# The last softmax chunk joins the row sums through an adding DMA; the additions around it change places in VectorE's queue

## The chip, the cores and the metric

The kernel runs on one core of a Trainium2 chip. The time is device microseconds (us) of one execution; several executions give a median. The profile is one further execution, recorded by the hardware profiler.

Engine names are those of the profile: PE is TensorE's matmul, PEld its weight load, DVE is VectorE, ACT is ScalarE, POOL is GpSimd, SP is SyncE. SP and POOL also issue the DMAs here. A queue name with a q (SPq, POOLq) is the part of an engine that issues instructions.

## The reference

The input is 16 images of 256 channels and 32x32 positions, in f32. Two layers follow each other, and each one does

```
x = x + attention(groupnorm(x))
```

The group norm has 16 groups along the last image axis, which the code treats as channels. The attention has 4 heads of 64 channels over 1024 tokens, and a position term made of queries:

```
q, k, v = Wq x + bq, Wk x + bk, Wv x + bv          # per head 64 x 1024
sim[i, j]  = q[:, i] . k[:, j]
qpos[i, j] = (rel_h + rel_w)[:, i] . q[:, j]
out        = v @ softmax(sim + qpos, axis=-1)^T
```

The layers have their own weights. Everything is computed in f32.

## The kernel before

**Units, blocks and chunks.** A unit is one layer of one image, 32 units in all; images alternate so that a layer of one is interleaved with a layer of another. A unit has four blocks, numbered b = 0 to 3: two pairs of heads, `pr`, by two halves of the 1024 queries, `half`. So b = 0 and 2 are *half-0 blocks*, and b = 1 and 3 are *half-1 blocks*. A block has eight chunks of 128 keys, j = 0 to 7. For each chunk:

- `seed` (L343, DVE) writes the position term, 128x1024, into a PSUM tile;
- `scores` (L379, PE) adds the product of keys and queries onto it, in 8 matmuls;
- the exponential (L388, ACT) leaves the probabilities in an SBUF tile `p`, 128x1024 f32.

`attend` (L413, PE) multiplies the probabilities by the values, in two stretches of 64 matmuls, `values_of_p(0)` and `values_of_p(1)`. Four PSUM tags of two banks each, a, b, c and d, carry everything; `ring` says which stage uses which. A seed can be written only when ACT has read what stood in its tag before.

**Row sums.** `add_up(blk, j)` (L397 for j = 1, L399 for j = 2 to 7, all on DVE) adds up the eight chunks of a block into a tile `acc`, 128x1024. The two last chunks of a block are partly added in the next block, where the code calls that block `previous`. Then, for all but the last four blocks (`folded`):

- `fold` (L432): an adding DMA, issued by POOL, adds partitions 64 to 127 of `acc` onto partitions 0 to 63 (256 KB);
- `stack_up` (L441): two plain DMAs, issued by SP, copy a quarter each into a tile `stack` (64 KB each);
- `fold_again` (L448): two adding DMAs, issued by POOL, add the next quarters onto them;
- `sums_of_pair` (L460, PE) forms the sums of a pair's two blocks at the end of the following half-0 block. ACT copies them (L475), SP sends them to `den_all` (L481), DVE takes reciprocals (L519), SP spreads those through DRAM over the partitions (L521, L526, tile `rden`), and `finish` (L538, L540, DVE) multiplies the output by them and adds bias and residual. `finish` runs in half-1 blocks only, before the seeds of the next block. In the second layer it also issues the output DMA (L542).

**Pieces.** Projections, values and position terms of the coming unit are cut into pieces and put between the chunks' scores: `first` and `second`, made by `prepare`. A piece has two stretches of matmuls, which use different rows of the array. Between two stretches stands a *word*: when the first stretch is done, POOL writes one element of a tile `token` (L163), and the second stretch waits for that. These words stand in POOL's queue in program order with the DMAs that POOL issues: the order there within a half-0 block is word of `first`, `fold`, word of `second`, `fold_again`, word of `attend`. In a half-1 block it is word of `first`, `fold`, word of `attend`, `fold_again`; the second piece of such a block has one stretch only.

**Group norm of the unit after the next.** ACT forms its sums and squares 1/16 at a time (`norm_sums`, `norm_squares`, L187, and `norm_apply`, L242), at written-out places between the exponentials. In block 3 `norm_var` ends with two small POOL operations (L231, L233). Every second unit or so, block 3 also loads an image (`load_x`, L106, 1 MB on SP's queue), 13 times in all after the start.

The order on every engine is the program's order: nothing is rearranged by a scheduler. PE's order of a block is scores 1 to 3 (their seeds were written in the block before), `first(0)`, scores 4, `second(0)`, `first(1)`, scores 5, `second(1)`, scores 6, scores 7, `values_of_p(0)`, scores 0 of the next block, `values_of_p(1)`. DVE's order of a half-1 block is add 7 of the previous block, seed 4, add 1, reciprocal, seeds 5, 6, 7, adds 2, 3, 4, seed 0 of the next block, add 5, `finish` (two operations), seeds 1, 2, 3 of the next block.

Of the kernel before, what the change touches and what calls it, by code (L numbers as in the profile page):

```python
# [13 lines left out]
ALU = mybir.AluOpType  # L14
# [5 lines left out]
G = 16  # L20
# [32 lines left out]
def fast_path(ctx, tc, sh, x, layers, out, W, den_all, token, good, flag):  # L53
# [26 lines left out]
    nc = tc.nc  # L80
    B, C, H, N, CC, NT, NH, D, GT = (
        sh.B, sh.C, sh.H, sh.N, sh.CC, sh.NT, sh.NH, sh.D, sh.GT
    )
# [19 lines left out]
    def load_x(b):  # L103
        xt[b] = xpool.tile([P, CC, N], F32, tag="x", name=f"x_{b}")
        for cc in range(CC):
            nc.sync.dma_start(xt[b][:, cc, :], flat(x[b, cc * P : (cc + 1) * P]))  # L106
# [39 lines left out]
    def psum2(tag, name):  # L146
        return ps_s.tile([P, 2, HALF], F32, tag=tag, name=name)
# [37 lines left out]
    def of_group(u, g, func, into, **bias):  # L185
        junk = small.tile([P, CC * sh.W, GT], F32, tag="junk", name=f"junk_{u}_{g}")
        nc.scalar.activation(  # L187
            junk, grouped(xt[units[u][0]], g), func, accum_out=into[:, g : g + 1], **bias
        )

    def norm_sums(u, gs):
        if u not in reds:
            reds[u] = small.tile([P, G], F32, tag="red", name=f"red_{u}")
        for g in gs:
            of_group(u, g, AF.Identity, reds[u])
# [26 lines left out]
    def norm_squares(u, gs):  # L222
        for g in gs:
            of_group(u, g, AF.Square, sums[u], bias=negs[u][:, g : g + 1])
# [14 lines left out]
    def norm_apply(u, gs):  # L239
        rstd, shift = rss[u]  # L240
        for g in gs:
            nc.scalar.activation(  # L242
                grouped(xns[u], g),
                grouped(xt[units[u][0]], g),
                AF.Identity,
                bias=shift[:, g : g + 1],
                scale=rstd[:, g : g + 1],
            )
# [87 lines left out]
    seeds, probs, accs, outs = {}, {}, {}, {}  # L336
# [18 lines left out]
    def widen(u, pr):  # L355

        r = W.rel[units[u][1]][:, pr, :]
        t = gnpool.tile([P, CC, N], F32, tag="gn", name=f"wide_{u}_{pr}")[:, 0, :]
        nc.vector.tensor_tensor(
            t.rearrange("p (w y) -> p w y", y=H),  # L360
            r[:, :H].unsqueeze(1).to_broadcast([P, sh.W, H]),
            r[:, H:].unsqueeze(2).to_broadcast([P, sh.W, H]),
            ALU.add,
        )
        wide[u, pr] = t

    def scores(blk, j, tag=None):

        u, pr, half = blk
        ps = psum2(tag, f"ps_{u}_{pr}_{half}_{j}") if tag else seeds.pop((blk, j))  # L370
        columns = slice(half * HALF, (half + 1) * HALF)
        for x, c in enumerate(QUARTERS):
            for h, hs in enumerate(QUARTERS):
                j0 = j * P + x * D
                terms = [(ks[u, pr], qs[u, pr])]
                if tag:
                    terms = [(qs[u, pr], wide[u, pr])] + terms
                for i, (a, b) in enumerate(terms):
                    nc.tensor.matmul(  # L379
                        ps[c, h, :],  # L380
                        a[hs, j0 : j0 + D],
                        b[hs, columns],
                        start=bool(tag) and i == 0,
                        stop=i == len(terms) - 1,
                        skip_group_check=True,
                    )
        p = ppool.tile([P, 2, HALF], F32, tag="p", name=f"p_{u}_{pr}_{half}_{j}")
        nc.scalar.activation(p, ps, AF.Exp, bias=W.shift)  # L388
        probs[blk, j] = p

    def add_up(blk, j):
        u, pr, half = blk
        if j == 0:
            return
        if j == 1:
            accs[blk] = apool.tile([P, 2, HALF], F32, tag="acc", name=f"acc_{u}_{pr}_{half}")
            nc.vector.tensor_tensor(accs[blk], probs[blk, 0], probs[blk, 1], ALU.add)  # L397
        else:
            nc.vector.tensor_tensor(accs[blk], accs[blk], probs[blk, j], ALU.add)  # L399
# [26 lines left out]
    R = P // 4  # L426
    stacks = {}

    def fold(blk):

        acc = accs[blk]
        nc.gpsimd.dma_start(acc[:D], acc[D:], accum_op=ALU.add)  # L432
# [185 lines left out]
    def block(n):  # L618
        blk = blocks[n]
        u, b = divmod(n, BPU)  # L620
        half = blk[2]
        before = blocks[n - 3][:2] if half == 1 and n > 2 else None
        after = blocks[n + 1] if n + 1 < len(blocks) else None
        previous = blocks[n - 1] if n > 0 else None
        one, two = u + 1 < NU, u + 2 < NU

        pieces = u + 1 < NU or b < 2
        if u + 1 == NU and b == 1:
            widen(u, 1)
        f0, f1, f2, f3 = ring  # L630
        folded = n - 1 < FOLDED
        if not pieces:
            return block_without_pieces(n, half)

        if previous:
            add_up(previous, 6 if half == 0 else 7)
        for j in range(1, 4):
            scores(blk, j)
        if b == 3 and u + 3 < NU and units[u + 3][0] not in xt:
            load_x(units[u + 3][0])  # L640
        (first, first_out), (second, second_out) = prepare(u, b)
        first(0)
        if b == 0 and one:
            norm_apply(u + 1, range(0, 1))
        if b == 2 and two:
            norm_sums(u + 2, range(8, 11))
        if b == 3 and two:
            norm_squares(u + 2, range(6, 9))
        seed(blk, 4, f1)
        if previous and half == 0:  # L650
            add_up(previous, 7)
        scores(blk, 4)
        add_up(blk, 1)
        if before:
            reciprocals(*before)
        if half == 0:
            add_up(blk, 2)
        if b == 0 and one:
            norm_apply(u + 1, range(1, 5))
        if b == 1 and one:  # L660
            norm_apply(u + 1, range(15, G))
        if b == 2 and two:
            norm_sums(u + 2, range(11, G))
        if b == 3 and two:
            norm_squares(u + 2, range(9, 13))
        second(0)
        if half == 1:
            second_out()
        first.word()
        if previous and folded:  # L670
            fold(previous)
            stack_up(previous)
        first(1)
        first_out()
        seed(blk, 5, f0)
        scores(blk, 5)
        if half == 0:
            add_up(blk, 3)
            second.word()
            if previous and folded:  # L680
                fold_again(previous)
            second(1)
            second_out()
        seed(blk, 6, f1)
        scores(blk, 6)
        if half == 0:
            ring[2:] = f3, f2
        seed(blk, 7, ring[2])
        scores(blk, 7)
        if half == 1:  # L690
            add_up(blk, 2)
            add_up(blk, 3)
        add_up(blk, 4)

        if after:
            seed(after, 0, f0)
        if n in check:
            next(checks)
        if b == 0 and one:
            norm_apply(u + 1, range(5, 10))  # L700
        if b == 3 and two:
            norm_squares(u + 2, range(13, G))
        po = psum2(ring[3], f"po_{n}")
        values_of_p = attend(blk, po)
        values_of_p(0)
        if two and b >= 2:
            mean, mean_out = (norm_mean if b == 2 else norm_var)(u + 2, zeroed(f1, f"pm_{n}"))
            mean(0)
        if after:
            scores(after, 0)  # L710
        values_of_p.word()
        if two and b >= 2:
            mean(1)
        if previous and folded and half == 1:
            fold_again(previous)
        if two and b >= 2:
            mean_out()
        add_up(blk, 5)
        if before:
            finish(*before)  # L720
        if half == 0:
            add_up(blk, 6)
        if after:
            for j in range(1, 4):
                seed(after, j, ring[j % 3])
        if b == 0 and one:
            norm_apply(u + 1, range(10, 15))
        if b == 1 and two:
            norm_sums(u + 2, range(0, 8))
        if b == 2 and two:  # L730
            norm_squares(u + 2, range(0, 6))
        values_of_p(1)
        if half == 1:
            take_out(blk, po)
            pos[n] = po
            return
        if n > 1:
            sums_of_pair(*blocks[n - 2][:2], po)
        take_out(blk, po, n > 1)
# [477 lines left out]
```

## Time and profile before

| what | value |
|---|---|
| median of 3 runs | 2670.57 us (2669.98 to 2670.76) |
| the profiled execution: its own time | 2669.75 us |
| the profiled execution: span of the trace | 2667.9 us |
| mean granted TensorE clock | 0.999 |
| PE busy | 2608.5 us (98%) |
| DVE busy | 2407.3 us (90%) |
| ACT busy | 1992.4 us (75%) |
| POOL busy | 466.5 us (17%) |
| chain that ended last | PE 56%, DVE 29%, ACT 8%, issue 5%, DMA 3% |

Busy time is the time in which an engine has an instruction under way. Matmuls overlap, and their ends are modelled, so a stretch of PE is best measured from the start of one group to the start of the next. The chain that ended last follows the work back from the end, at each step to whatever released it. In the timeline each row is a group of like instructions: start, duration from the first start to the last end, engine, line, operation, tiles and count, and in brackets the idle time before it with what ended it.

The trace is very regular: from the unit at 381 us on, the copies of the half outputs (L485) come again after 22.50, 17.78, 22.80 and 19.20 us, which makes 82.28 us per unit.

### The profile page before, as it was taken

The page shows a single profiled execution, that of the slowest core. Times are in us where ns is not written, and L with a number is a line of the kernel's source. Part 1 is how long each engine was busy: PE and PEld are TensorE (multiplying, and loading weights), DVE is VectorE, ACT ScalarE, POOL GpSimd, SP SyncE. Part 2 cuts the span into 40 slices and gives each one's busy share as a digit, 9 for nine tenths or more (in the row PEclk, how much of TensorE's full clock was granted, in tenths as well). Part 3 has the DMA queues.
Part 4 walks back from the last instruction along what each step waited for, and adds up shares of the span by engine and source line. Part 5 has one row for each costly group of instructions (what it writes and reads, how often), then busy time and mean ns, then how long its engine had stood idle before and what let it go on. Part 6 is the DMA issues. An engine that isn't in the chain of part 4 may idle for free.

```text
span 2667.9 us, 86560 instructions
## 1 busy us (share of the span) xinstructions
PE 2608.5 (98%) x37970; PEld 1412.8 (53%) x37970; DVE 2407.3 (90%) x2200; ACT 1992.4 (75%) x3996; POOL 466.5 (17%) x825
## 2 busy tenths in 40 slices
PE   8999999999999999999999999999999999999998
PEld 4555455555555555555545555455555555554554
DVE  7988988989989899898998998998989989899998
ACT  6778777787777777777777778777777777777754
POOL 1211211112112111121121111211112112111110
PEclk9999999999999999999999999999999999999999
DMA  2222231322322223222222222222222232222221
GB/s 80 36 58 44 40 73 34 69 52 36 73 40 67 49 35 77 44 59 50 53 61 42 58 51 62 52 42 58 55 58 51 42 68 47 49 43 47 50 51 46
DMA packets 76136, 140.26 MB, mean 53 GB/s; under 512 B 33896, under 2 KB 35432, under 8 KB 75752
## 3 DMA queue, kind: packets, MB, share of 16 engines
q0 software_dynamic: 21824, 48.78, 12.6%
q1 hardware_dynamic: 53928, 85.89, 11.2%
q8 instruction: 299, 4.90, 0.8%
q14 instruction: 85, 0.70, 0.1%
HBM read 51.78 MB, written 17.30 MB: 26 GB/s over the span
## 4 chain that ended last, share of the span: by engine, by line
PE 56%; DVE 29%; ACT 8%; issue 5%; DMA 3%; SPq 0%; POOL 0%; DVEq 0%; POOLq 0%
PE ps L379 18%; PE po L413 17%; DVE ps L343 11%; DVE acc L399 10%; PE pq L262 8%; PE pk L262 6%; PE pv L292 4%; DVE x L540 3%; DVE od L538 3%; ACT p L388 3%; ACT junk L187 2%; ACT abt L331 2%; DMA den_all<-od 2%; DVE acc L397 1%; PE po L460 1%
## 5 line engine op out<-in xcount | busy, mean ns | idle before, releaser
L388 ACT ACTIVATE p<-ps,shift 128x1024 f32<-128x1024 f32 x1024 | 1105.4, 1118 | 428.7 <-PE ps L379 264.3
L343 DVE TENSOR_TENSOR ps<-abt 128x1024 f32<-128x1024 f32 x1018 | 1219.9, 1226 | 221.1 <-ACT p L388 116.2
L379 PE MATMUL ps<-q,k 64*64 64x512 f32 x8192 | 1038.7, 598 | 28.6 <-DVE ps L343 22.9
L399 DVE TENSOR_TENSOR acc<-acc,p 128x1024 f32<-128x1024 f32 x768 | 936.6, 1220 | 16.6 <-ACT p L388 0.9
L413 PE MATMUL po<-p,v 64*64 64x256 f32 x16384 | 933.5, 377 | 0.0
L413 PEld LDWEIGHTS po<-p,v 64*64 64x64 f32 x16384 | 674.0, 133 | 289.6 <-issue 61.4
L379 PEld LDWEIGHTS ps<-q,k 64*64 64x64 f32 x8192 | 296.4, 132 | 500.6 <-DVE ps L343 334.6
L163 POOL MEMSET token<- 1x1 f32 x380 | 33.8, 89 | 1795.0 <-PE po L413 696.0
L448 POOL DMA_DIRECT2D stack<-acc x248 | 195.0, 921 | 303.0 <-DMA stack<-acc 267.8
L292 PE MATMUL pv<-Wv,xn 64*64 64x256 f32 x4096 | 247.2, 376 | 0.3 <-DVE var L865 0.3
L262 PE MATMUL pq<-xn,Wq 64*64 64x512 f32 x2048 | 243.4, 590 | 0.3 <-DVE xn L897 0.3
L262 PE MATMUL pk<-xn,Wk 64*64 64x512 f32 x2048 | 242.9, 589 | 0.0
L292 PEld LDWEIGHTS pv<-Wv,xn 64*64 64x64 f32 x4096 | 176.5, 133 | 80.4 <-issue 49.7
L242 ACT ACTIVATE xn<-x,nshift,rstd 128x128 f32<-128x128 f32 x496 | 210.4, 497 | 0.1
L187 ACT ACTIVATE junk<-x,neg 128x128 f32<-128x128 f32 x498 | 197.0, 407 | 1.0
L397 DVE TENSOR_TENSOR acc<-p,p 128x1024 f32<-128x1024 f32 x128 | 155.6, 1216 | 0.0
L262 PEld LDWEIGHTS pq<-xn,Wq 64*64 64x64 f32 x2048 | 78.6, 134 | 141.7 <-issue 140.1
L187 ACT ACTIVATE junk<-x 128x128 f32<-128x128 f32 x480 | 144.1, 306 | 2.6 <-DVE x L540 2.6
L262 PEld LDWEIGHTS pk<-xn,Wk 64*64 64x64 f32 x2048 | 75.5, 134 | 123.5 <-issue 115.3
L485 ACT COPY od<-po 128x512 f32<-128x512 f32 x127 | 74.7, 589 | 75.5 <-PE po L413 75.5
L432 POOL DMA_DIRECT2D acc<-acc x124 | 103.4, 834 | 71.9 <-DVE acc L399 41.5
L231 POOL TENSOR_TENSOR rstd<-var,mhalf 128x16 f32<-128x16 f32 x30 | 108.2, 3607 | 3.2
(78 smaller groups left out, 1060.0 us busy)
## 6 DMA issues: line engine op xcount, KB each, us to landing
rden<-rd SPq DMA_DIRECT2D x126, 256.0 KB
acc<-acc POOLq DMA_DIRECT2D x124, 256.0 KB, 3.6
x<-in_x_dram SPq DMA_DIRECT2D x32, 512.0 KB
stack<-acc SPq DMA_DIRECT2D x248, 64.0 KB
stack<-acc POOLq DMA_DIRECT2D x248, 64.0 KB, 2.6
out_dram<-x SPq DMA_DIRECT2D x31, 512.0 KB
den_all<-od SPq DMA_DIRECT2D x124, 4.0 KB
rd<-r SPq DMA_DIRECT2D x63, 8.0 KB
```

Source lines behind the costliest of these rows:

```text
L187: nc.scalar.activation(junk, grouped(xt[units[u][0]], g), func, accum_out=into[:, g : g + 1], **bias)
L231: nc.gpsimd.tensor_tensor(rstd, var, W.mhalf[:, :G], ALU.pow)
L242: nc.scalar.activation(grouped(xns[u], g), grouped(xt[units[u][0]], g), AF.Identity, bias=shift[:, g : g + 1], scale=rstd[:, g : g + 1],)
L262: yield nc.tensor.matmul(pk[c, nh, :], w[l][rs, cc, c0 : c0 + D], xns[u][rs, cc, nh * HALF : (nh + 1) * HALF], start=(t == 0 and cc == 0), ...
L292: yield nc.tensor.matmul(pv[c, a, i, :], xns[u][rs, cc, j0 : j0 + D], W.wv[l][rs, cc, :], start=(t == 0 and cc == 0 and i == 0), stop=(t = ...
L343: nc.vector.tensor_tensor(ps.rearrange("p h (w y) -> p h w y", y=H), ab[:, :, :H].unsqueeze(2).to_broadcast([P, 2, XH, H]), ab[:, :, H + h ...
L379: nc.tensor.matmul(ps[c, h, :], a[hs, j0 : j0 + D], b[hs, columns], start=bool(tag) and i == 0, stop=i == len(terms) - 1, skip_group_check ...
L388: nc.scalar.activation(p, ps, AF.Exp, bias=W.shift)
L397: nc.vector.tensor_tensor(accs[blk], probs[blk, 0], probs[blk, 1], ALU.add)
L399: nc.vector.tensor_tensor(accs[blk], accs[blk], probs[blk, j], ALU.add)
L413: yield nc.tensor.matmul(po[c, a, :QUART], vts[u][rs, j, c0 : c0 + D], p[rs, h, a * QUART : (a + 1) * QUART], start=(t == 0 and j == 0), s ...
L448: nc.gpsimd.dma_start(stacks[u, pr][r0 : r0 + R, :], acc[R:D, h, :], accum_op=ALU.add)
```

## The change

The eighth chunk of a block (j = 7) is no longer added by DVE, for all blocks but the last four: a new function `add_last` issues a DMA on POOL's queue that adds the whole tile `p` (128x1024, 512 KB) onto `acc`. It is issued at the start of the next block, after add 6 of the previous block, which in every block now opens DVE's work. The `fold` that follows reads what this DMA wrote.

The other additions move: add 2 stands between seeds 5 and 6 in every block, and adds 3 and 4 after seed 7. Before, in a half-0 block, add 2 stood ahead of seed 5, add 3 between seeds 5 and 6, and add 6 behind add 5; in a half-1 block adds 2, 3 and 4 all stood after seed 7. `finish` stays where it was relative to the seeds, behind add 5. On ACT two of the sixteen squares of block 3 move from ahead of `second_out` to behind the eighth exponential.

```diff
+    def add_last(blk):
+        nc.gpsimd.dma_start(accs[blk], probs[blk, NT - 1], accum_op=ALU.add)
+
...
         if previous:
-            add_up(previous, 6 if half == 0 else 7)
+            add_up(previous, 6)
+            if folded:
+                add_last(previous)
+            else:
+                add_up(previous, 7)
         for j in range(1, 4):
             scores(blk, j)
...
         seed(blk, 4, f1)
-        if previous and half == 0:
-            add_up(previous, 7)
         scores(blk, 4)
         add_up(blk, 1)
         if before:
             reciprocals(*before)
-        if half == 0:
-            add_up(blk, 2)
...
         if b == 3 and two:
-            norm_squares(u + 2, range(9, 13))
+            norm_squares(u + 2, range(9, 11))
...
         seed(blk, 5, f0)
         scores(blk, 5)
+        add_up(blk, 2)
         if half == 0:
-            add_up(blk, 3)
             second.word()
             if previous and folded:
                 fold_again(previous)
...
         seed(blk, 7, ring[2])
         scores(blk, 7)
-        if half == 1:
-            add_up(blk, 2)
-            add_up(blk, 3)
+        add_up(blk, 3)
         add_up(blk, 4)
...
         if b == 3 and two:
-            norm_squares(u + 2, range(13, G))
+            norm_squares(u + 2, range(11, G))
...
         add_up(blk, 5)
         if before:
             finish(*before)
-        if half == 0:
-            add_up(blk, 6)
         if after:
```

## The prediction

> **What bounds the kernel now.** I read the page first, for the busy shares, the chain that ended last and the DMA issues, then the timelines of one half-1 block (b = 3) on PE and DVE, and last POOL's timeline in the half-0 block before it.
>
> ```profile
> span 2667.9 us, 86560 instructions
> ...
> PE 2608.5 (98%) x37970; PEld 1412.8 (53%) x37970; DVE 2407.3 (90%) x2200; ACT 1992.4 (75%) x3996; POOL 466.5 (17%) x825
> ...
> PE 56%; DVE 29%; ACT 8%; issue 5%; DMA 3%; SPq 0%; POOL 0%; DVEq 0%; POOLq 0%
> ...
> acc<-acc POOLq DMA_DIRECT2D x124, 256.0 KB, 3.6
> ```
>
> PE looks full at 98%, yet DVE holds 29% of the chain: somewhere PE waits for it in small steps. PE's timeline shows where:
>
> ```profile
> 1089.57 1.09 PE L379 MATMUL ps<-q,k 64*64 64x512 f32 x8 [0.56 <-DVE ps L343]
> 1090.48 3.63 PE L413 MATMUL po<-p,v 64*64 64x256 f32 x64
> 1094.47 0.23 PE L207 MATMUL pm<-sum,avg 64*64 64x16 f32 x2 [0.36 <-DVE pm L199]
> ...
> 1095.47 3.68 PE L413 MATMUL po<-p,v 64*64 64x256 f32 x64
> 1099.12 3.36 PE L379 MATMUL ps<-q,k 64*64 64x512 f32 x24
> 1102.29 1.91 PE L292 MATMUL pv<-Wv,xn 64*64 64x256 f32 x32
> ```
>
> From start to start, unhindered groups take 0.86 us for a chunk's scores, 1.72 for a piece's stretch, 3.45 for half of attend, 0.93 for the position terms, 0.43 for the sums. Against those, PE loses 0.78 us before scores 7 (the group ahead, scores 5 and 6, began at 1087.07 and needed 1.72), 0.54 before the norm's `pm`, 0.20 before the three scores at 1099.12, and 0.59 inside them (3.17 where 2.58 are needed): **2.1 us** in block 3. In block 1 the same count gives 0.37 + 0.60 = **1.0 us**. The half-0 blocks between them have gaps of 0.1 us at most: they are bound by PE. So about 3.1 us of a unit's 82.28 can be had.
>
> DVE in the same block:
>
> ```profile
> 1085.84 1.23 DVE L343 TENSOR_TENSOR ps<-abt 128x1024 f32<-128x1024 f32 x1 [0.56 <-ACT p L388]
> 1088.28 1.23 DVE L343 TENSOR_TENSOR ps<-abt 128x1024 f32<-128x1024 f32 x1 [1.20 <-ACT abt L331]
> 1089.42 3.74 DVE L399 TENSOR_TENSOR acc<-acc,p 128x1024 f32<-128x1024 f32 x3
> 1093.08 1.23 DVE L343 TENSOR_TENSOR ps<-abt 128x1024 f32<-128x1024 f32 x1
> 1094.23 1.21 DVE L399 TENSOR_TENSOR acc<-acc,p 128x1024 f32<-128x1024 f32 x1
> ...
> 1097.81 3.52 DVE L343 TENSOR_TENSOR ps<-abt 128x1024 f32<-128x1024 f32 x3
> 1101.24 1.23 DVE L399 TENSOR_TENSOR acc<-acc,p 128x1024 f32<-128x1024 f32 x1
> ```
>
> DVE idles 1.76 us for seeds 6 and 7, then three additions hold back seed 0 of the next block, and everything behind it is late.
>
> [...] Back to back, starts are 1.14 us apart, which I use. [...] `fold` lands after 3.6 us alone, but `stack_up` starts 5.5 us after it (1084.47 to 1089.99) beside the reciprocals' spreading.
>
> **The change, part by part.**
>
> *DVE loses 124 additions,* 124 x 1.22 = 151 us of busy time. But block by block: a half-0 block had additions 6 and 7 of the previous and 1 to 6 of its own, and keeps six of these eight. A half-1 block has six before and six after (6 of the previous for 7). All that is removed lies in blocks that PE bounds: **worth nothing directly**; PE's work covers it.
>
> *The new order in the half-1 block is what pays.* Block 3, on the times above: seed 5 ends at 85.2; add 2 fills the gap to 86.35; seed 6 to 87.5 (0.5 later than before, hidden: PE scores 5 until 87.93). Seed 7 needs the copy of `abt`, which started at 1087.26 behind four squares of 0.39 us; two move behind it, so it ends 0.78 earlier, at 87.4. Seed 7: 87.5 to 88.64, in time for scores 7 at 88.79. Adds 3 and 4 end at 90.9, seed 0 at 92.1. PE then goes 89.65, attend to 93.1, `pm` and scores 0 to 94.1, attend to 97.55. DVE: add 5, `finish`, then seed 1 at 95.6 (`pm`'s tag must first be read by ACT), seed 3 ends 99.1, when scores 3 are due at 99.27. The next piece starts at 1100.1 instead of 1102.29: 2.1 us. Block 1, worked likewise: seed 0 about 1.0 earlier, gain 1.0. The moved squares fall into ACT's 2.38 us of idleness ahead of the next exponential: nothing. Some 30 units: 30 x 3.1 = **-93 us**.
>
> *124 DMAs of 512 KB are added.* POOL: 124 x 0.82 (`fold`'s row) = 102 us, in a queue that is 17% busy. Landing: the page gives 48.78 MB on that queue 12.6% of 16 engines' span, 336 us, so 0.5 MB takes 3.6 us and `fold`'s half 1.8; `fold` lands after 3.6, hence 5.4. From the sizes instead (64 KB 2.6, 256 KB 3.6) it is 4.9. I take **L = 5.15**. [...] the upper one is `fold`'s longest landing, 6.5, plus 1.6 = 8.1.
>
> *A wait is added:* `fold` now stands in POOL's queue until the new DMA has landed, and the word of `second` stands behind it. Before:
>
> ```profile
> 1062.55 0.09 POOL L163 MEMSET token<- 1x1 f32 x1 [7.63 <-PE pq L262]
> 1063.40 0.81 POOL L432 DMA_DIRECT2D acc<-acc  x1 [0.77 <-DVE acc L399]
> 1065.12 0.09 POOL L163 MEMSET token<- 1x1 f32 x1 [0.91 <-PE pk L262]
> 1069.35 1.57 POOL L448 DMA_DIRECT2D stack<-acc  x2 [4.13 <-DMA stack<-acc]
> ```
>
> In a half-0 block, from the start of scores 1: `second(1)` is due after 2.58 + 1.72 + 0.86 + 1.72 + 1.72 + 0.86 = 9.46 us. Add 6 ends after 2.7 to 2.8; the DMA starts 0.3 later; then L, and 1.2 for `fold`'s issue, the word and the signals. So the word is in time while L is below some **5.2**: a margin of nothing. I charge 0.3 us for blocks 0 and 2 together, 30 x 0.3 = **+9 us**. `fold_again` and the word of attend, moved later by the same chain, have over 1 us left, and the sums' use of `stack` 2 us. SP's `stack_up` gets later too; behind it stand only `den_all` and output stores, not due then. In half-1 blocks no word stands between `fold` and attend's, so POOL can wait.
>
> *DMA against DMA:* in 13 of the blocks 3 an image (1 MB) is loaded just when the new DMA runs; the reciprocals' trip (L521, L526) queues behind the image on SP. If the engines' times add, the trip lands 1.5 to 3 us later and `finish`, which has about 0.5 us to spare once the block is shorter, holds seeds 1 to 3. Nothing shows this overlap; from 0 to 2.5 us, I take 1.5: 13 x 1.5 = **+20 us**.
>
> Sum: -93 + 9 + 20 = -64 on the profiled execution's 2669.75 us (span 2667.9 and 1.85 around it); the median is 0.8 above that execution: **2606 us**.
>
> **The rivals.**
> 1. *The DMAs cost nothing* (L under 5, image loads overlap freely): 2670.6 - 93 = 2577 us. For it: the DMA engines are about a quarter busy. Against: the margin is nil.
> 2. *POOL's wait becomes the bound, and the kernel slower.* Each us of L beyond 5.15 stops PE for 1 us at `second(1)` in some 61 half-0 blocks. It decides from L = 5.15 + 93/61 = 6.7. At 8.1: 61 x 2.95 = 180 - 93, so 2758. For it: `fold` has taken 6.5. Against: it did so in half-1 blocks beside the reciprocals' spreading, which half-0 blocks don't have.
> 3. *Seed 7 stays behind ACT's copy,* or another release: then only one addition less lies ahead of seed 0, and block 3 gains 1.1 instead of 2.1: 30 us less, 2636.
> 4. That the additions were not worth removing because PE is at 98%: same time, 2670. Against: the gaps counted above.
>
> **How the numbers follow.** Forecast 0.55, rival 1 0.20, rival 3 0.10, rival 2 0.13 (a little of it within the bound), rival 4 0.02. A measurement of this kernel tells about 0.2%, 5.3 us, from no change. Faster 0.84, within 0.04, slower 0.12. The range goes from 2572, rival 1 with a little more, to 2655, rival 3 with L = 5.45 (18 us more); only rivals 2 and 4 and odd ends lie outside.
>
> **What would show it.** Right: blocks 1 and 3 near 17.7 and 18.3 us of PE work, `DVE ps L343` gone as an idle cause of PE, the new DMA landing near 5.2, DVE 150 us less busy. The token wait shows as PE idle for POOL L163 before the piece's second stretch; the image's cost as DVE waiting for `rden` in every second block 3. Wrong: PE waiting for words over 1.5 us per half-0 block, or the half-1 blocks as long as now.

## The result, and the profile after

The changed kernel takes **2683.35 us** (median of 10 runs, 2676.64 to 2691.70) against 2669.99 us for the kernel before (10 runs): ratio **1.0051** (95% interval 1.0039 to 1.0062). It is slower by half a per cent where 2606 us was forecast. The profiled execution took 2683.82 us, its span is 2682.0.

The page after, in the lines that answer to those of before:

```profile
span 2682.0 us, 86789 instructions
...
PE 2595.6 (97%) x37970; PEld 1410.4 (53%) x37970; DVE 2261.4 (84%) x2076; ACT 1986.3 (74%) x3996; POOL 565.7 (21%) x949
...
PE 61%; DMA 16%; DVE 10%; issue 5%; ACT 4%; POOL 2%; SPq 1%; DVEq 0%; POOLq 0%
...
acc<-p POOLq DMA_DIRECT2D x124, 512.0 KB, 4.7
```

DVE has lost its 146 us, and its share of the chain fell from 29% to 10%. What took its place stands in the same line: DMA went from 3% to 16%. The new DMA itself lands after 4.7 us, sooner than the 5.15 that the forecast took.

The time between the last copies of successive blocks (L485 before, L488 after) tells where the time went. All are us from the timelines, means over units 4 to 25; a unit with a load is one whose block 3 loads an image, and what that costs shows in the block 0 that follows.

| block | before | after |
|---|---|---|
| 0, following a load | 22.50 | 26.04 |
| 0, others | 22.49 | 22.64 |
| 1 | 17.79 | 18.47 |
| 2 | 22.81 | 22.14 |
| 3 | 19.20 | 18.14 |

Block 3 has its gain, and block 2 part of its own (in both, the seeds at the end of a half-1 block come earlier). Block 1 is longer, and the blocks 0 that follow a load lose 3.5 us each. The other blocks 0 do not lose, but they do not gain either, so that a unit without a load takes 81.4 us: 0.9 us less than before, where 3.1 were forecast. Where nothing disturbs it, PE's timeline from block 3 into block 0 is as forecast; here in a unit without a load:

```profile
1268.66 0.23 PE L207 MATMUL pm<-sum,avg 64*64 64x16 f32 x2
...
1269.67 3.66 PE L413 MATMUL po<-p,v 64*64 64x256 f32 x64
1273.14 2.77 PE L379 MATMUL ps<-q,k 64*64 64x512 f32 x24
1275.73 1.91 PE L292 MATMUL pv<-Wv,xn 64*64 64x256 f32 x32
```

The three scores take 2.59 us from start to start instead of 3.17, and attend runs on into them without a gap. The largest loss is in the units with a load. There SP, POOL, DVE and PE show one chain, each in its own timeline:

```profile
1170.14 0.90 SPq L106 DMA_DIRECT2D x<-in_x_dram  x2
1172.99 0.33 SPq L524 DMA_DIRECT2D rd<-r  x1
1179.52 1.19 SPq L529 DMA_DIRECT2D rden<-rd  x2
```

```profile
1170.83 0.89 POOL L430 DMA_DIRECT2D acc<-p  x1 [7.07 <-ACT p L388]
...
1179.60 0.83 POOL L435 DMA_DIRECT2D acc<-acc  x1 [6.80 <-DMA acc<-p]
```

```profile
1186.19 1.23 DVE L541 TENSOR_TENSOR od<-od,rden 128x1024 f32<-128x1024 f32 x1 [3.96 <-DMA rden<-rd]
```

```profile
1183.25 3.66 PE L413 MATMUL po<-p,v 64*64 64x256 f32 x64
1189.94 4.59 PE L379 MATMUL ps<-q,k 64*64 64x512 f32 x24 [3.03 <-DVE ps L343]
```

The image and the adding DMA start within 0.7 us of each other, and the latter takes 8.8 us instead of 4.9. The reciprocals' `rd`, 8 KB issued 2.2 us behind it, answers after 6.5 us, so `rden` is late, `finish` waits 3.96 us in DVE's queue, the seeds behind it are late, and PE stops for 3.03 us. Over the whole trace `finish` waits for `rden` 20 times, where it never did before, and PE's wait for seeds is twice the 22.9 us of before (us in total, times, longest):

```profile
DVE od L541 <- DMA rden<-rd: 53.6, 20, 4.5
PE ps L379 <- DVE ps L343: 45.6, 45, 3.6
```

And then PE's three scores take 4.59 us instead of 2.8. Some 0.6 us of that is the seeds, which come every 1.14 us where a chunk's scores need 0.86; the rest is the clock, which was halved. In stretches of the same core (the clock stands behind POOL's busy time):

```profile
1186.00:1189.50 3.50, 0.91 (x20) 0.36 (x10) 3.27 (x3) 0.58 (x1) 0.34 (x1) 1.00 0.17 42
1189.50:1192.90 3.40, 2.92 (x20) 0.88 (x24) 3.40 (x4) 1.15 (x2) 2.37 (x3) 0.78 0.66 195
1192.90:1196.30 3.40, 3.40 (x44) 1.71 (x40) 3.26 (x4) 2.70 (x3) 3.32 (x3) 0.72 0.00 0
```

(0.22 + 0.28) x 3.4 = 1.7 us of full speed are missing there, an upper bound of what is lost, since PE also waits a little in them. The trace has seven such drops, each to half speed for 3.41 us, at most seven times 1.7 = 12 us, and none in the kernel before. They go with stops of PE, but the length of a stop does not tell which: after the kernel's start PE has nine stops of 2.0 to 3.6 us, and seven of them have a drop within or just behind them, among these the shortest, of 2.01 us, while two, of 2.52 and 3.05 us, have none.

In block 1 it is another small transfer that is held, the sums' way to `den_all`. POOL, SP and DVE:

```profile
1294.68 0.89 POOL L430 DMA_DIRECT2D acc<-p  x1 [4.75 <-DVE acc L399]
...
1299.58 0.81 POOL L435 DMA_DIRECT2D acc<-acc  x1 [0.61 <-DMA acc<-p]
```

```profile
1295.11 1.18 SPq L484 DMA_DIRECT2D den_all<-od  x2
```

```profile
1299.67 0.25 DVE L522 RECIPROCAL r<-den_all 128x16 f32<-128x16 f32 x1 [0.69 <-DMA den_all<-od]
```

`den_all` is issued 0.4 us behind the adding DMA, and what waits for it goes on 0.1 us after what waits for the DMA. The reciprocal, and with it seed 5, is 0.7 us late here, and block 1 is 0.7 us longer in the mean.

### The profile page after: what moved, and what is told of

Read it like the earlier page. It is cut to its first block, busy times and chain, and to the rows that moved or that the text cites. A ratio compares the mean times of both kernels' runs of the same rounds, so it can differ in the third digit from the quotient of the medians.

```text
span 2682.0 us, 86789 instructions
## 1 busy us (share of the span) xinstructions
PE 2595.6 (97%) x37970; PEld 1410.4 (53%) x37970; DVE 2261.4 (84%) x2076; ACT 1986.3 (74%) x3996; POOL 565.7 (21%) x949
## 4 chain that ended last, share of the span: by engine, by line
PE 61%; DMA 16%; DVE 10%; issue 5%; ACT 4%; POOL 2%; SPq 1%; DVEq 0%; POOLq 0%
PE po L413 26%; PE ps L379 19%; PE pq L262 7%; DMA den_all<-od 6%; DVE ps L343 5%; PE pk L262 4%; PE pv L292 4%; DMA rd<-r 4%; DMA rden<-rd 4%; ACT p L388 2%; DVE acc L399 1%; ACT od L488 1%; DVE acc L397 1%; ACT junk L187 1%; PE po L463 1%
## 5 line engine op out<-in xcount | busy, mean ns | idle before, releaser
L343 DVE TENSOR_TENSOR ps<-abt 128x1024 f32<-128x1024 f32 x1018 | 1225.8, 1228 | 317.3 <-ACT p L388 123.2
L413 PEld LDWEIGHTS po<-p,v 64*64 64x64 f32 x16384 | 658.7, 133 | 306.8 <-issue 58.8
L399 DVE TENSOR_TENSOR acc<-acc,p 128x1024 f32<-128x1024 f32 x644 | 784.4, 1218 | 5.3 <-ACT p L388 0.5
L379 PEld LDWEIGHTS ps<-q,k 64*64 64x64 f32 x8192 | 313.4, 133 | 480.9 <-DVE ps L343 258.4
L430 POOL DMA_DIRECT2D acc<-p x124 | 111.9, 903 | 536.9 <-ACT p L388 360.6
L163 POOL MEMSET token<- 1x1 f32 x380 | 50.8, 134 | 704.2 <-PE po L413 474.5
L488 ACT COPY od<-po 128x512 f32<-128x512 f32 x127 | 74.7, 589 | 75.0 <-PE po L413 75.0
```

The costliest lines, as they stand in the source:

```text
L343: nc.vector.tensor_tensor(ps.rearrange("p h (w y) -> p h w y", y=H), ab[:, :, :H].unsqueeze(2).to_broadcast([P, 2, XH, H]), ab[:, :, H + h ...
L379: nc.tensor.matmul(ps[c, h, :], a[hs, j0 : j0 + D], b[hs, columns], start=bool(tag) and i == 0, stop=i == len(terms) - 1, skip_group_check ...
L413: yield nc.tensor.matmul(po[c, a, :QUART], vts[u][rs, j, c0 : c0 + D], p[rs, h, a * QUART : (a + 1) * QUART], start=(t == 0 and j == 0), s ...
L430: nc.gpsimd.dma_start(accs[blk], probs[blk, NT - 1], accum_op=ALU.add)
```

## The experiments

Each was compared with the kernel before, run beside it on the same chip (2670.1 to 2670.2 us). The theory from the two traces (theory 1): the new order of the additions gives the whole gain; the DMA gives only losses, by what is queued or running beside it. The first four runs test it from both ends.

**order_only.** The kernel before, with these edits alone:

```
-            norm_squares(u + 2, range(9, 13))
+            norm_squares(u + 2, range(9, 11))
...
             second_out()
+        else:
+            add_up(blk, 2)
         seed(blk, 6, f1)
...
         if half == 1:
-            add_up(blk, 2)
             add_up(blk, 3)
```

(and the last squares from 11 on). 

> The kernel before with the new order of the half-1 blocks alone: add 2 between seeds 5 and 6, adds 3 and 4 after seed 7, two squares of block 3 moved behind the eighth exponential. No adding DMA of 512 KB; all eight chunks are added by DVE, and the half-0 blocks are as before. Theory 1 (the order gives the gain, the DMA only costs): blocks 1 with 2 lose 1.0 us and blocks 3 with 0 lose 2.0 us, 30 x 3 = 90 us, less up to 15 short drops of the granted clock at 1.7 us each: 2580 to 2606 us. Theory 2 (the gain of the quiet units comes from taking additions off DVE): half-0 blocks stay too full on DVE, and the time is 2640 us or more.

Measured: 2588.51 us, ratio 0.9693 (0.9677 to 0.9709). The gain needs no addition to be taken off DVE; theory 2 falls.

**dma_half0.** The changed kernel with

```
-            add_up(previous, 6)
-            if folded:
-                add_last(previous)
+            if half == 0:
+                add_up(previous, 6)
+                if folded:
+                    add_last(previous)
...
+        if half == 0:
+            add_up(blk, 6)
```

and add 7 on DVE at the start of half-1 blocks. 

> The changed kernel, with the adding DMA of 512 KB only where the previous block is a half-1 block (62 DMAs, all issued in half-0 blocks); the half-0 block's chunks are all added by DVE, add 6 in its own block and add 7 at the start of the next, as before. Theory 1 (the loss is the DMA's meeting with the sums' and reciprocals' transfers and the image loads in half-1 blocks): those are gone, so the same time as order alone, 2580 to 2606 us, and a spread of the runs below 2 us. Rival (the loss is the wait of fold and the second token in half-0 blocks): the 62 waits stay, and the time stays above 2650 us.

Measured: 2600.04 us, ratio 0.9735 (0.9719 to 0.9752); the runs spread over 5.6 us, more than expected. The 62 waits of `fold` in half-0 blocks are no big loss; the rival falls. (One drop of the clock is in this trace, after a stop of 2.11 us for a word.)

**load_behind.** The changed kernel, with `load_x` moved from ahead of the pieces to behind `reciprocals`. 

> The changed kernel with the image load of block 3 issued on SP after the reciprocals' trip (rd, rden) instead of ahead of it; all 124 adding DMAs stay. Theory 1 (the trip waits in SP's queue behind an image that shares the DMA engines with the adding DMA): finish no longer waits for rden, the 13 units with a load lose their 4 to 5 us, 2625 to 2640 us. Rival (the trip is late because the adding DMA itself holds the engines): rden stays late and the time stays above 2665 us.

Measured: 2673.26 us (2661.35 to 2687.05 in 18 runs), ratio 1.0011 (1.0001 to 1.0021): outside what theory 1 gave. The image is no longer ahead of `rd`, yet `rd` answered after 3.2 us in the median with a load and 2.8 without (1.4 before, without a load). The image then met `rden` and `fold`: `finish` still waited up to 3.3 us, and PE's matmuls waited for words 40 us in all, against 17 us in the changed kernel. The time is the one that the rival gave. So the order in SP's queue is not enough to explain the loss; but as the image met other transfers instead, the run tells no more than that.

**load_block2.** `load_x` behind `fold_again` in block 2. 

> The changed kernel with the image load moved into block 2, behind fold_again, where no adding DMA of 512 KB runs; all 124 adding DMAs stay. Theory 1: as with the load behind the trip, the collision is gone, 2620 to 2640 us, and the runs spread by less than 3 us. Rival (the 4 to 5 us in these units come from elsewhere, for instance from the drops of the clock): no change, 2675 to 2690 us.

Measured: 2641.53 us (2638.74 to 2642.20), ratio 0.9891 (0.9875 to 0.9908), and no drop of the clock. The meeting of the image and the adding DMA costs 2683.4 - 2641.5 = **42 us**, the drops among it. Block 1 stays at 18.46 us.

**dma_only.** The kernel before, with add 7 done by the DMA and nothing moved. 

> The kernel before, with addition 7 of each folded block done by the adding DMA of 512 KB and nothing else moved: add 6 stays in its own half-0 block, adds 2, 3 and 4 of the half-1 blocks stay after seed 7, all squares stay. DVE loses the same 124 additions (151 us). Theory 1 (taking additions off DVE is worth nothing, and the DMA costs through the transfers behind it): about 22 us from 13 units with an image load, up to 15 us from the late sums in blocks 1, little back: 2675 to 2710 us. Theory 2 (the relief of DVE itself is worth something): below 2660 us.

Measured: 2678.55 us (2672.99 to 2681.36), ratio 1.0030 (1.0021 to 1.0040). As theory 1 said, though not by its reasons: `rd` and `den_all` answered as before (1.42 and 3.79 us). Here add 6 stays in its own half-0 block, so the DMA goes out 4.6 us before that block's last copy, and, at the 4.7 us to landing of the changed kernel, is about to land when `den_all` goes. That led to the last experiment.

**squares_unmoved.** order_only without the move of the squares. 

> Order alone without the adding DMA, as in the earlier run of that order, but the two squares of block 3 stay ahead of the copy of abt. The prediction's rival 3 in reverse: seed 7 of block 3 then waits for that copy 0.78 us longer, and seed 0, pm and all behind it are 0.8 us later: 30 x 0.8 = 24 us, about 2612 us. If the squares don't matter: 2588 us.

Measured: 2604.73 us, ratio 0.9753 (0.9737 to 0.9769). The squares are worth 16 us, not 24.

**order_all.** No adding DMA of 512 KB; the changed kernel's order of adds 2, 3 and 4 in both kinds of block, adds 6 and 7 where they were. 

> No adding DMA of 512 KB; all additions on DVE, with add 2 between seeds 5 and 6 and adds 3 and 4 after seed 7 in both kinds of block (add 7 stays behind seed 4 and add 6 behind add 5 in half-0 blocks). Small gaps of 0.1 us before scores 5 of the half-0 blocks should go, since seed 5 no longer stands behind add 2: 60 x 0.1 = 6 us, 2580 to 2588 us. If DVE in the half-0 blocks is too full for it, the time is above 2590 us.

Measured: **2578.36 us** (2577.31 to 2580.17), ratio **0.9657** (0.9641 to 0.9673): the fastest kernel here, 1.6 us under the expected range. It is 10 us faster than order_only, so the order within the half-0 blocks pays too. Its page:

```profile
PE 2554.3 (99%) x37970; PEld 1418.9 (55%) x37970; DVE 2399.9 (93%) x2200; ACT 1976.5 (77%) x3996; POOL 476.6 (19%) x825
...
PE 84%; ACT 9%; DVE 3%; DMA 2%; issue 1%; SPq 0%; POOL 0%; DVEq 0%; ACTq 0%; POOLq 0%
```

DVE is as busy as before the change, 2400 us, and is 3% of the chain instead of 29%. dma_half0 differs from it only in who adds chunk 7 in half-0 blocks, so 62 adding DMAs cost 2600.0 - 2578.4 = 22 us, 0.35 us each. Their waits show as idle time of PE's weight loads, which wait for words, first in dma_half0, then in order_all:

```profile
PEld pq L262 <- POOL token L163: 24.8, 31, 3.0
...
PEld pk L262 <- POOL token L163: 19.5, 30, 1.8
```

```profile
PEld pq L262 <- POOL token L163: 0.5, 1, 0.5
```

Most of the 62 waits cost nothing. In units 4 to 25 of dma_half0, 9 of the 44 half-0 blocks have an adding DMA that lands after 5.9 to 6.7 us, and these take 0.9 to 1.6 us more than the median block. It is one us for each us of landing beyond about 5.2 us in blocks 0, and beyond 4.9 in blocks 2.

**block1_later.** load_block2, with

```
-            if folded:
+            if folded and b != 1:
...
         first.word()
         if previous and folded:
+            if b == 1:
+                add_last(previous)
             fold(previous)
```

> The kernel with the image load in block 2, and in blocks 1 alone the adding DMA issued after the word of first instead of at the block's start, so that the sums' transfer to den_all is ahead of it and the reciprocals' rd behind it. If a small transfer issued behind the adding DMA signals only when that has landed (what blocks 3 show: rd answers within 0.1 us of it), then den_all is back at 3.8 us from 4.6, rd takes some 4 to 5 us in blocks 1 instead of 1.5, and rden is late: block 1 gains up to 0.7 us and gives back part, 2620 to 2645 us. If the small transfers only share bandwidth, rd stays near 2 us and the time is near 2618 us.

Measured: 2616.95 us, ratio 0.9801 (0.9785 to 0.9818): 25 us less than load_block2. Block 1 takes 17.66 us, and `den_all` 3.79. `rd` did not take 4 us but 1.45: the assumption that it would be issued behind the DMA was wrong, it went out 0.24 us ahead of it. The run confirms the cost of the held `den_all` (0.8 us in each of 31 blocks 1 makes the 25); on `rd` in block 1 it tells nothing.

**half1_later.** block1_later, with the same for block 3 (`if half == 1`). 

> As the kernel with the image load in block 2 and block 1's adding DMA behind the word of first, but now block 3's too: in all half-1 blocks the adding DMA is issued behind that word, about when the reciprocals' rd is, no longer 2.2 us ahead of it. Theory A (rd answers late only because it is issued behind a running adding DMA, with which it lands to 0.1 us): rd answers after 1.4 to 2.0 us in block 3 instead of 3.0. Theory B (rd is late because the engines are shared while both run): rd stays near 3 us. For the time: fold, stack_up and fold_again of block 3 come 2 to 3 us later and push the norm's POOL operations and block 0's adding DMA: 2617 to 2660 us.

Measured: 2666.75 us (2659.53 to 2673.64), ratio 0.9981 (0.9966 to 0.9997). `rd`, issued 0.25 us ahead of the DMA, answers after 1.41 us in the median of blocks 3, as theory A has it. In the changed kernel it is issued 2.2 us behind, and in 24 of 31 blocks 3 the two answers fall within 0.2 us of each other, though `rd`'s came anywhere from 2.4 to 7.3 us after its issue.

The packets show that more than `rd`'s signal is late. `rd` is 128 packets of 64 bytes and 16 signals on SP's queue q1; the adding DMA runs on q0. In the changed kernel, first the 1.84 us after an `rd` was issued at 429.40, then the 0.36 us that follow; last, the first 1.09 us after an `rd` in order_all (packets, MB, share of the 16 DMA engines' time):

```profile
q0 software_dynamic: 89, 0.36, 104.1%
```

```profile
q1 hardware_dynamic: 144, 0.01, 30.2%
q8 instruction: 1, 0.02, 19.1%
q0 software_dynamic: 16, 0.00, 6.5%
```

```profile
q1 hardware_dynamic: 144, 0.01, 8.5%
```

So here the data of `rd` itself do not move until the adding DMA begins to signal that its own are through. Without a DMA ahead its first packet moves 0.82 us after the issue (median of the changed kernel); behind one, in all 17 such blocks 3 of the changed kernel without an image and all 27 of load_block2, it moves within 0.01 us of the DMA's first signal, in the former 1.89 us after the issue (median). With an image beside them it moves 3.6 to 4.2 us after the issue, from 1.0 us ahead of that signal to 1.3 us behind it. In block 1 `den_all` is late in its packets too: half of them have moved 3.9 us after the issue (median) instead of 1.6. That is neither a late signal alone nor a shared rate (theory B).

The time came out 7 us over what was expected. It shows another chain, which hangs on how early block 3's DMA is issued. From the waits of this run:

```profile
PEld pq L262 <- POOL token L163: 78.5, 31, 5.0
PE pq L262 <- POOL token L163: 50.7, 27, 4.1
ACT xn L242 <- POOL nshift L233: 44.1, 26, 3.9
```

The norm's two POOL operations stand behind `fold_again`, and block 0's adding DMA and word behind those. In the changed kernel that chain hardly shows: ACT waits there for `nshift` 3.6 us in all.

**block3_dve.** block1_later, with add 7 of the block before on DVE in block 3 (and add 6 of block 2 at that block's own end). 

> As the kernel with the image load in block 2 and block 1's adding DMA behind the word of first, but the addition of chunk 7 that falls into block 3 is done by DVE as before (93 adding DMAs are left: in blocks 0, 1 and 2). If the rest of the half-1 blocks' loss is block 3's chain (the DMA, fold, stack_up, fold_again, the norm's two POOL operations, then block 0's DMA and word), the time falls from 2617 to about 2600 us, that of the kernel whose adding DMAs stand in half-0 blocks only. If it is block 1's: about 2617 us as before.

Measured: 2594.61 us, ratio 0.9716 (0.9700 to 0.9732): block 3's DMA cost 22 us even without an image beside it. This is not the chain over the norm that was expected, for PE's matmuls wait for the word of `pq` 6.5 us in block1_later and 6.7 us here. What goes is the wait of `finish`, first in block1_later, then here:

```profile
DVE od L541 <- DMA rden<-rd: 16.5, 16, 2.8
```

```profile
DVE od L541 <- DMA rden<-rd: 0.2, 1, 0.2
```

`rd` answers after 2.84 us in the median of block1_later's blocks 3 and after 1.41 here, so it is the late `rd` again, without an image.

**image_twice.** order_all with each image of block 3 loaded twice. 

> No adding DMA of 512 KB at all: the kernel with the new order in both kinds of block and every addition on DVE (2578 us), with the image of block 3 loaded twice, one load behind the other, so that the reciprocals' trip waits on SP's queue some 4 us longer in the 13 blocks that load one. Theory (the trip's lateness alone makes the loss of those blocks): rden arrives about 4 us later, PE stops about 3 us before block 0's scores, the following block 0 takes 25 to 27 us instead of 21.6, the granted clock drops to half for 3.4 us after some of these stops, and the time is 2620 to 2645 us. If the adding DMA itself is needed for the loss, or for the clock's drops: below 2595 us, no drops.

Measured: 2647.52 us, ratio 0.9918 (0.9902 to 0.9935), 2.5 us over what was expected. No adding DMA of 512 KB, and yet the same picture:

```profile
DVE od L542 <- DMA rden<-rd: 54.1, 13, 6.2
PE ps L383 <- DVE ps L347: 42.4, 13, 5.3
```

13 waits of `finish`, 13 stops of PE, the following block 0 at 26.85 us, and 11 drops of the clock. So a late `rden` is enough for the loss of these units, and for the drops (two of them twice as long): they follow PE's stops, and need no such DMA.

**add6_own.** The changed kernel with one thing undone, the place of add 6:

```
-            add_up(previous, 6)
+            if half == 0:
+                add_up(previous, 6)
             if folded:
                 add_last(previous)
...
             finish(*before)
+        if half == 0:
+            add_up(blk, 6)
```

> The changed kernel with one thing undone: add 6 of a half-0 block stays at the end of its own block, so that in half-1 blocks the adding DMA is ready some 4 us earlier and can land before the sums' den_all, the image load and rd are issued. All 124 adding DMAs stay, and the image load stays in block 3. Theory (the half-1 blocks' loss comes from the place of add 6, which puts the DMA ahead of the small transfers and on top of the image): den_all answers after 3.8 us, rd after 1.4, and the time is that of the kernel with adding DMAs in half-0 blocks only, 2595 to 2610 us. Rival (124 such DMAs are too many wherever they stand): above 2640 us.

Measured: 2594.76 us (2592.98 to 2594.98), ratio 0.9715 (0.9699 to 0.9731), with all 124 adding DMAs and the image where it was. `den_all` answers after 3.79 us, `rd` after 1.42 without a load, and there is no drop of the clock. Two blocks 3 of this kernel, POOL in one without a load and SP in one with a load:

```profile
1208.28 0.89 POOL L430 DMA_DIRECT2D acc<-p  x1 [0.45 <-issue]
...
1217.26 0.83 POOL L435 DMA_DIRECT2D acc<-acc  x1 [0.38 <-issue]
```

```profile
1292.28 1.17 SPq L484 DMA_DIRECT2D den_all<-od  x2
1293.50 0.91 SPq L106 DMA_DIRECT2D x<-in_x_dram  x2
1296.34 0.33 SPq L524 DMA_DIRECT2D rd<-r  x1
1298.53 1.91 SPq L529 DMA_DIRECT2D rden<-rd  x2
```

The DMA goes out 9 us ahead of `fold`, which no longer waits for it, and `rd` answers after 2.2 us behind an image here (3.5 in the median; 3.2 in the kernel before). So the loss in half-1 blocks is not the DMA's size or number, but that add 6, put at the head of the next block, makes it ready just when the small transfers and the image go out. That DVE has one addition less at the head of these blocks is not the reason: block3_dve has one there in block 3, block1_later in block 1, and these blocks are as short.

## Why the prediction was wrong

The sum was -93 + 9 + 20 = -64. Measured by the runs it is -92 + 22 + 42 + 42 = +13 (order_all; dma_half0 over that; load_block2 over that; the changed kernel over that; as each step starts where the last one ended, the total comes out by construction).

- *PE is the bound of the half-0 blocks, DVE of the tails of the half-1 blocks, 3.1 us of a unit can be had:* **right** in place and size. order_all needs 79.3 us per unit where 82.28 were needed: -3.0. That -93 meets -92 so closely is partly luck: the half-1 order alone, which the -93 stood for, gave 82 us (order_only), and 10 more came from the half-0 blocks, which had no term.
- *The 124 additions are worth nothing, the order pays:* **right**. order_all has them all and is the fastest; dma_only lacks them and gains nothing.
- *Rival 3's term, the squares:* right in kind; 16 us instead of 24 to 30.
- *L = 5.15:* a little high; 4.7 us to landing in the median, about 4.9 from issue to `fold`'s issue in blocks 0.
- *The wait ahead of the second word, +9 us:* right in mechanism, mis-sized. Its threshold of about 5.2 us is what dma_half0 shows (5.2 in blocks 0, 4.9 in blocks 2). But one value of L was taken for all blocks: the median block lands after 4.6 to 4.7 us and loses nothing, and most of the 22 us comes from the blocks in which L reached 5.9 to 6.7 us. Why it does so in these is open.
- *The image, 13 x 1.5 = +20 us:* **mis-sized**. The 1.5 us was an estimate that no trace showed. Chain and place were right (image, `rd`, `rden`, `finish`, seeds), but 42 us are lost. The adding DMA took 8.9 us in the median there, `rd` came with it, and seven of PE's nine stops of 2.0 to 3.6 us went with 3.41 us at half clock on top, which no part of the sum had.
- *"In half-1 blocks no word stands between `fold` and attend's, so POOL can wait":* **this step failed**. It is true of POOL's words, and it was taken as if the DMA were free there but for the image. The working followed POOL's queue, but never set the adding DMA's start beside the start of SP's small transfers, so this cost stood at nothing. Two of them were late behind the DMA, in their packets: half of `den_all`'s had moved 3.9 us after its issue instead of 1.6, and the first of `rd`'s moved, without an image, 1.89 us after its issue instead of 0.82. `den_all` in block 1, issued 0.4 us behind the DMA, cost block 1's gain (25 us by block1_later). And `rd` in block 3, issued 2.2 us behind it, held `finish` and block 0 even without an image (22 us by block3_dve). Together without the image that is 42 us, by load_block2 against dma_half0; the two steps together make 47, and where the 5 us of difference lie is open.

Rival 2 had the sign, but not the reason: it needed L above 6.7 us in the half-0 blocks, and their median stayed at 4.9 to 5.0. The range was too narrow because the half-1 blocks had no term but the image's. Of the signs that the prediction named, block 1 "as long as now" came true (18.47 us against 17.79), and `DVE ps L343` as an idle cause of PE did not go but doubled; in order_all it is gone.

## What to carry to other kernels

When work is moved from an engine to a DMA, ask when that DMA becomes ready, and which small transfers go out in the microseconds behind it: here the place of one addition, which looked like a detail, was worth 89 us (2683.4 against 2594.8). Before that, ask whether the engine needs relief at all: filling an idle gap ahead of a seed with one addition, and moving one more and two squares behind the seeds, gave 92 us with every addition still in place. And a wait that stops PE is priced with the clock that can go with it: here seven of nine stops of 2.0 to 3.6 us had a drop, at up to 1.7 us each.

## What the hardware showed unexpectedly

- A stop of PE of some 2 to 5 us can go with 3.41 us at half clock (up to 1.7 us lost): 7 times in the changed kernel's trace, 11 in image_twice, none in order_all or before. Not every stop has one (two of nine in the changed kernel have none), and what decides it is open. The changed kernel's runs spread over 15 us where those of before spread over 1.3; mean clock and time go together from run to run (0.996 at 2676.64 us, 0.992 at 2691.70).
- A transfer of 8 KB issued 2.2 us behind one of 512 KB on another queue answered within 0.2 us of it in 24 of 31 cases; issued 0.25 us ahead of it, it answered after 1.41 us. Behind the large one, without an image, its first packet moved 1.9 us after its issue instead of 0.82, together with the large one's first signal.
